# A two-layer graph network: attention formed inside the second edge pass, and gathered rows as three bf16 parts

## The chip, the cores and the metric

One core of a Trainium2 chip runs the kernel. The metric is device microseconds of one execution; the times of a kernel are given as the median of several runs. A profiled execution has a time of its own and a span, which is the time from its first to its last recorded instruction.

## The reference: what is computed

The graph has N = 12500 nodes with 256 features and E = 200000 edges (`src`, `dst`), sorted by `dst`. Two blocks follow each other, each with a residual:

```
h = relu(layernorm(x))
# block 1: two graph convolutions, self loops included
h = h @ W_pre + b_pre
h = relu(conv(h, W1, b1)); h = relu(conv(h, W2, b2))
x = x + h @ W_post + b_post          # conv: out[d] = sum over edges (s, d) of norm * (h @ W)[s]
# block 2: attention, 4 heads of 64
h = relu(layernorm(x)); xt = (h @ weight).reshape(N, 4, 64)
alpha = softmax over heads(leaky_relu(xt[src] . attn_l + xt[dst] . attn_r))
tmp[n] = sum over heads of alpha[n] * xt[dst[n]]      # alpha and dst of edge n, for n < N
x = x + tmp, repeated for each of the 4 heads
```

In block 2 only the first N edges count: node n takes the scores of edge n. As `dst` is sorted, the destinations of these 12500 edges are among the first nodes (under 1152), while their sources are spread over all nodes. So the term with `attn_l`, the left score, of an edge may belong to any node, also to one that is finished last.

## The kernel before: how the work is laid out

**Passes.** After a preparation (loads, degree counts, layer norms, a table of rows in DRAM, `table1`) come two edge passes, both made by `convolve` (L1153). Edges are cut into 112 chunks (`NCH`) of 14 tiles (`J`) of 128 edges, 1563 tiles in all. The loop at L1365 goes over tiles. For each tile GpSimd's queue (Pool) gathers 128 rows of the table by the edges' sources with one indirect DMA (L1374), and TensorE multiplies a one-hot matrix (`fhot`, made for a whole chunk by `one_hots`, L1239) by these rows and adds the product to `acc` in PSUM (L1382), f32 by f32. A row has 260 f32 (1040 bytes) in pass 1 and 256 (1024 bytes) in pass 2. Rows land in a ring of chunk buffers named `fgot`: five in pass 1 (`new_got`, L533), four in pass 2 (`new_rows_of`, L1251, with `ahead` 4). In pass 1 the first four chunks come from `x` itself, gathered in the preparation (L668).

**Windows.** A chunk's sums are turned and added (`close`, `turn`, `add`, from L1273) into a moving buffer over the sorted destinations. When a window of 128 nodes is complete, `shift` takes the steps that `finish` returned. There are 98 windows (`NT`). The steps of pass 1 are `finish1` (L1410): the weights, relu, and a row block stored to `table2` by ScalarE's queue (L1423). Those of pass 2 are `finish2` (L1464): the weights of the second convolution (L1472), W_post (L1488), the residual stored to `kept_x` (L1495), layer norm, a transpose (L1514), and the attention's products (L1527), from which the left scores go to DRAM tables `table_l` and `table_e` (L1536, L1538), and for the first nine windows (`XW`) the rows and right scores to `table_r`.

**Order.** The kernel is written with an order made by hand: every engine runs its instructions in the order of the program. A step is entered by `at` (L1167) with the tile count at which it is due, and `run(t)` (L1183) emits what is due behind each tile's matmul. So the work of windows is strewn between tiles. In the last chunks (`near`, L1278) the distances shrink to one tile a step. Waits follow from the tiles and tables that instructions read and write; the first chunk of pass 2 gathers only from `table[:(NT - TW) * P]`, the rows but for the last two windows, and edges with sources in these two are added by `late_sums` (L1256), which takes one chunk buffer of the ring.

**Attention.** Two groups' end rows are formed in the pass (`ends`, `copied`, L1551 and L1556). The rest comes behind the last window, in the block from L1605: for 15 groups of up to 7 node tiles, `ends_of` (L1638) forms the rows of destinations by products with one-hots `hot_t` (made by `turn_hots`, L1570, from destinations loaded to all partitions); `mix` (L1656) gathers the left scores with one indirect DMA a node tile (L1662, 98 in all), then softmax over heads, the weighted sum over heads on DVE (L1685 to L1692), the residual (L1694), and the store to `out` (L1700). For the first chunk of edges the sources in the last three windows are added by products (`missing`, L1627, with `hot_l`).

**Fallback.** Counts are checked on the chip; if one fails, `tile_preln_gcn_gat_kernel` (L1714) runs `general_path` behind the fast path.

Of the kernel before, what the change touches and what calls it, by code (L numbers as in the profile page):

```python
# [10 lines left out]
I32 = mybir.dt.int32  # L11
# [402 lines left out]
def fast_path(  # L414
# [57 lines left out]
    table2 = dram.tile([NT * P, D], F32, name="ftable2")  # L472
    kept_x = dram.tile([NT * P, D], F32, name="kept_x")
# [3 lines left out]
    assert AC * J == NT and AC * CE <= E and XW < NT  # L477
    table_r = dram.tile([XW * P, DR], F32, name="table_r")
    table_l = dram.tile([NT * P, H], F32, name="table_l")

    LW = 3
    table_e = dram.tile([NT * P, H], F32, name="table_e")
# [18 lines left out]
    base_b = const.tile([P, NCH], F32, name="base_b")  # L501
    row_i = const.tile([P, AC], I32, name="row_i")
# [88 lines left out]
    with tc.tile_pool(name="fprep", bufs=1) as prep:  # L591
# [233 lines left out]
        with tc.tile_pool(name="fpsum", bufs=2, space=PSUM) as psum, \  # L825
# [227 lines left out]
            wide = prep.tile([NCH, P], F32, name="wide")  # L1053
            nc.vector.tensor_copy(wide, base.to_broadcast([NCH, P]))
# [7 lines left out]
            nc.tensor.matmul(fk[:, 2, :NCH], wide, ident[:NCH, :NCH], start=True, stop=True)  # L1062
# [7 lines left out]
            for f in after:  # L1070
                f()
            after = [raw_block(ends, m, psum.tile([P, 4 * P], F32, name="ft"), j0)
                     for j0 in (8, 12)]
            nc.vector.tensor_copy(base_b, fk[:, 2, :NCH])
            nc.vector.tensor_scalar(row_i, base_b[:, :AC], lane, float(XW * P - 1), op0=ALU.add,
                                    op1=ALU.min)
# [16 lines left out]
    def check_chunks(work, psum):  # L1093
# [20 lines left out]
        kept = work.tile([1, 1], F32, name="n_kept", bufs=1)  # L1114
        nc.vector.tensor_reduce(kept, pt[:1, 2, :NCH], AX.X, ALU.add)
        nc.vector.tensor_add(kept, kept, counted)
        nc.vector.tensor_scalar(bad_row, kept, -1.0, float(NCH + 1), op0=ALU.mult, op1=ALU.add)
# [12 lines left out]
    def load_late(pool):  # L1130

        nc.scalar.dma_start(roots, root_t)
        for t, w in ((wb, w2), (wo, w_post), (wg[:, :, :D], w_gat)):
            nc.scalar.dma_start(t, w.rearrange("(k p) n -> p k n", p=P))
        nc.scalar.dma_start(b2c, b2.rearrange("(k p) -> p k", p=P))
# [8 lines left out]
    def late_weights(pool, attn):  # L1144

        for i, ar in enumerate(attn):
            for k in range(KC):
                prod = pool.tile([P, H, C], F32, name="fprod", bufs=1)
                nc.vector.tensor_mul(prod.rearrange("p h c -> p (h c)"), wg[:, k, :D], ar)
                nc.vector.tensor_reduce(wg[:, k, D + i * H:D + (i + 1) * H], prod, AX.X,  # L1150
                                        ALU.add)

    def convolve(ep, table, stride, width, ahead, with_sum, psum, prepare, finish, lacking=False,  # L1153
                 raw=(), rows_p=None):
# [28 lines left out]
        def run(now=None):  # L1183

            while due:
# [3 lines left out]
                do(d)  # L1189

# [41 lines left out]
        const_p = psum.tile([P, P if with_sum else P + D], F32, name="iota_p", bufs=1)  # L1232
        iota_p = const_p[:, :P]
        nc.vector.tensor_copy(iota_p, iota_w)
        if not with_sum:
            state["bias"] = const_p[:, P:]
            nc.vector.tensor_copy(state["bias"], bob)

# [4 lines left out]

        def hot_of(c):

            n = nj[c]
            h = ep.tile([P, J, P], F32, name="fhot", bufs=3)
# [3 lines left out]
        def new_rows_of():  # L1251
            if with_sum:
                return new_got()
            return rows_p.tile([P, J, stride], F32, name="fgot", bufs=ahead)

        def late_sums():  # L1256

            h = ep.tile([P, J, P], F32, name="fhot", bufs=3)
# [5 lines left out]
            px = psum.tile([P, KC, P], F32, name="fpt", bufs=1)  # L1264
# [8 lines left out]
        def close(c, acc, t):  # L1273
# [4 lines left out]
            near = c + 3 >= NCH  # L1278
# [20 lines left out]
            def shift(now):  # L1299
# [31 lines left out]
                for i, (o, step, fills) in reversed(list(enumerate(steps))):  # L1331
                    then = at(now + (i + 1 if near else o), lambda _, step=step: step(), fills, then)
# [32 lines left out]
        for t, (c, j) in enumerate(tiles):  # L1365
# [3 lines left out]
            if j == 0:  # L1369
                gots = (raw + [spare])[c] if raw and c <= len(raw) else new_rows_of()  # L1370
            got = gots[:, j, :]
            some = lacking and c == 0
            if c >= len(raw):
                nc.gpsimd.indirect_dma_start(  # L1374
                    out=got, out_offset=None, in_=table[:(NT - TW) * P, :] if some else table[:],
# [377 lines left out]
```

## Time and profile before

| | |
|---|---|
| median of 4 runs | 4150.29 us (4150.09 to 4151.45) |
| the profiled execution | 4146.63 us, its span 4144.8 us |
| Pool | 3103.8 us busy (75%), 3299 instructions |
| TensorE | 3096.9 us busy (75%), mean granted clock 0.799 |
| VectorE (DVE) | 1139.8 us busy (28%) |
| ScalarE (ACT) | 491.8 us busy (12%) |
| DMA | 554.57 MB, mean 134 GB/s |
| first tile gather (L1374) | 131.7 us |
| last tile gather ends | 3983.6 us |
| first and last score gather (L1662) | 4002.1 and 4125.4 us |

How to read it: a group's line names the source line, engine, operation, the tile written and those read, shapes and count; behind the bar stand the busy time, the mean duration in ns, and the idle time just before these instructions with what ended most of it ("issue": nothing that the profile shows). A timeline's line has start, duration, engine, line and operation, and in brackets the idle time before it and its releaser. PEld is the load of weights into TensorE; a name with q (SPq, ACTq, DVEq) is the engine's queue. Pool's indirect DMA is counted while descriptors are made; the transfer itself comes behind it.

### The profile page before, as it was taken

How to read it: one execution, taken by the hardware profiler on the slowest of the kernel's cores; microseconds unless marked ns; L12 is line 12 of the kernel's file. 1: busy time of each engine (PE TensorE's matmuls, PEld its weight loads, DVE VectorE, ACT ScalarE, POOL GpSimd, SP SyncE). 2: the span in 40 equal slices, each digit the busy share in tenths (PEclk: the TensorE clock that was granted, in tenths of full speed). 3: DMA queues.
4: the chain of work that ended last, by engine and by line, in shares of the span. 5: the costliest groups of instructions: out<-in, count | busy, mean ns of one | idle time of the engine just before them, and what ended most of it. 6: DMA issues, size and time to landing. Idle time of an engine off the chain costs nothing. (4 is left out here: it accounts for less than half of the span.)

```text
span 4144.8 us, 32267 instructions
## 1 busy us (share of the span) xinstructions
PE 3096.9 (75%) x10600; PEld 1970.8 (48%) x10600; DVE 1139.8 (28%) x2421; ACT 491.8 (12%) x1233; POOL 3103.8 (75%) x3299
## 2 busy tenths in 40 slices
PE   6688787877778888777587777777777777777774
PEld 5464443444444444444365555554555545555552
DVE  8632111111111111111232222222222222222238
ACT  5400000000000000000011111111111111111122
POOL 7677777777777777777777777777777777777766
PEclk7697878777887777778688888788888888888876
DMA  8644444444444444444545544555555445444556
GB/s 271 197 127 122 118 119 120 122 120 120 120 123 120 120 120 122 118 119 120 151 125 134 129 128 127 128 132 128 128 128 132 128 127 128 129 125 128 132 165 203
DMA packets 327419, 554.57 MB, mean 134 GB/s; under 512 B 96301, under 2 KB 224836, under 8 KB 327244
## 3 DMA queue, kind: packets, MB, share of 16 engines
q0 software_dynamic: 153520, 414.16, 37.7%
q1 hardware_dynamic: 127878, 121.99, 9.8%
q10 hardware_dynamic: 45846, 16.27, 1.6%
q8 instruction: 87, 1.43, 0.1%
q14 instruction: 88, 0.72, 0.1%
HBM read 498.89 MB, written 53.21 MB: 133 GB/s over the span
## 5 line engine op out<-in xcount | busy, mean ns | idle before, releaser
L1374 POOL DMA_INDIRECT fgot<-ftable,fsrc_t x3056 | 2892.4, 946 | 945.5 <-issue 885.5
L1382 PE MATMUL facc<-fgot,fhot 128*128 128x257 f32 (+1 forms) x6252 | 2344.0, 495 | 885.4 <-DMA fgot<-ftable,fsrc_t 839.6
L1382 PEld LDWEIGHTS facc<-fgot,fhot 128*128 128x128 f32 x6252 | 1261.5, 232 | 1806.9 <-DMA fgot<-ftable,fsrc_t 1366.3
L1293 DVE TENSOR_TENSOR buf<-buf,fturn 128x256 f32 x224 | 94.4, 422 | 1632.9 <-PE fturn L1206 1295.5
L1241 DVE TENSOR_TENSOR fhot<-iota_p,to_t 128x1792 f32<-128x1792 f32 x224 | 448.9, 2004 | 4.4 <-PE fpt L1267 4.4
L1479 DVE SCALAR_TENSOR_TENSOR fy<-rb,fb2c,fpz 128x128 f32<-128x128 f32 x194 | 58.7, 344 | 733.8 <-PE fpz L1472 732.9
L1276 ACT ACTIVATE fsums<-facc 128x257 f32<-128x257 f32 (+1 forms) x224 | 86.0, 384 | 1154.5 <-PE facc L1382 1145.0
L1493 DVE SCALAR_TENSOR_TENSOR fx<-fpo,fdinv,fxb 128x256 f32<-128x256 f32 x97 | 46.9, 483 | 484.9 <-PE fpo L1488 484.9
L1417 PE MATMUL fpo<-wf,buf 128*128 128x256 f32 x388 | 153.8, 539 | 0.3 <-DVE buf L1293 0.3
L1422 ACT ACTIVATE fo<-fpo,fdinv 128x256 f32<-128x256 f32 x97 | 45.9, 473 | 747.6 <-PE fpo L1418 745.8
L1417 PEld LDWEIGHTS fpo<-wf,buf 128*128 128x128 f32 x388 | 112.3, 290 | 28.7 <-DVE buf L1293 0.8
L1472 PE MATMUL fpz<-buf,fwb 128*128 128x128 f32 x776 | 122.9, 310 | 0.0
L1472 PEld LDWEIGHTS fpz<-buf,fwb 128*128 128x128 f32 x776 | 120.4, 233 | 2.2 <-DVE fy L1479 0.3
L1488 PE MATMUL fpo<-fwo,fz 128*128 128x256 f32 x388 | 111.5, 412 | 0.1
L1206 PE MATMUL fturn<-fident,self 128*128 128x128 f32 x396 | 83.8, 297 | 36.6 <-DMA to_all<-in_src_dram 24.1
L1662 POOL DMA_INDIRECT fal<-table_l,fsrc_t x84 | 81.1, 966 | 25.6 <-issue 22.6
L1206 PE MATMUL fturn<-fident,fsums 128*128 128x128 f32 x448 | 95.2, 298 | 0.5 <-ACT fsums L1276 0.5
L1652 PE MATMUL fends<-rows,hot_t 128*128 128x260 f32 x168 | 67.1, 565 | 35.3 <-ACT fxg L1654 34.9
L1518 ACT ACTIVATE ht<-fpt 128x256 f32<-128x256 f32 x97 | 37.1, 383 | 464.2 <-PE fpt L1514 464.2
L668 POOL DMA_INDIRECT fgot<-in_x_dram,raw_i x56 | 73.2, 1307 | 15.4 <-issue 15.3
L1206 PEld LDWEIGHTS fturn<-fident,fsums 128*128 128x128 f32 x448 | 69.6, 156 | 30.7 <-issue 7.4
L1418 PE MATMUL fpo<-bb,fins 2*128 2x256 f32 x194 | 82.5, 510 | 0.0
(267 smaller groups left out, 1716.8 us busy)
## 6 DMA issues: line engine op xcount, KB each, us to landing
fgot<-ftable,fsrc_t POOLq DMA_INDIRECT x3056
self<-ftable SPq DMA_DIRECT2D x99, 128.0 KB
self<-ftable SPq DMA_DIRECT2D x97, 130.0 KB
ftable<-fo ACTq DMA_DIRECT2D x98, 128.0 KB
kept_x<-fx SPq DMA_DIRECT2D x98, 128.0 KB
fxb<-in_x_dram SPq DMA_DIRECT2D x97, 128.0 KB
fxr<-kept_x SPq DMA_DIRECT2D x13, 896.0 KB
out_dram<-fres SPq DMA_DIRECT2D x13, 896.0 KB
```

Of the source, the lines that this page charges most:

```text
L668: nc.gpsimd.indirect_dma_start(out=raw[c][:, j, :D], out_offset=None, in_=x[:], in_offset=bass.IndirectOffsetOnAxis(ap=raw_i[:, k:k + 1], ...
L1206: nc.tensor.transpose(v["pt"][:, i * KC + k, :], rows[:, k * P:(k + 1) * P], ident)
L1241: nc.vector.tensor_tensor(h, iota_p[:, None, :].to_broadcast([P, n, P]), to[:, :, None].to_broadcast([P, n, P]), ALU.is_equal)
L1276: nc.scalar.activation(sb, acc, AF.Copy)
L1293: nc.vector.tensor_add(b, b, v["pt"][:, :KC, :])
L1374: nc.gpsimd.indirect_dma_start(out=got, out_offset=None, in_=table[:(NT - TW) * P, :] if some else table[:], in_offset=bass.IndirectOffset ...
L1382: nc.tensor.matmul(acc, hots[c][:, j, :], got[:, :width], start=(j == 0), stop=(j == nj[c] - 1 and not some))
L1417: nc.tensor.matmul(po, buf[:, k, :P], wf[:, k, :], start=(k == 0), stop=False)
L1418: nc.tensor.matmul(po, fs, bb, start=False, stop=True)
L1472: nc.tensor.matmul(pz[:, m, :], wb[:, k, m * P:(m + 1) * P], buf[:, k, :P], start=(k == 0), stop=(k == KC - 1))
L1488: nc.tensor.matmul(po, v["z"][:, m, :], wo[:, m, :], start=(m == 0), stop=(m == KC - 1))
L1662: nc.gpsimd.indirect_dma_start(out=al[:, i, :], out_offset=None, in_=(table_l if c else table_e)[:], in_offset=bass.IndirectOffsetOnAxis(a ...
```

## The change

1. **Rows in parts.** `finish1` now leaves each row of `table2` also as three bf16 parts (value, rest, rest of the rest) in `parts2`; pass 2 gathers from there (1536 bytes a row) and multiplies each tile's one-hots, now bf16, by the three parts. In pass 1 `split_rows` does the same for `table1`, one window in three tiles from tile 70 on, into `parts1` (1560 bytes a row); chunks from the 29th on (`SINCE` = 28) use it. The ring of pass 2 has three chunk buffers in place of four.
2. **Attention by products.** Left scores stay on the chip (`l_all`); `table_l` and `table_e` are gone. `start_of` is a load of a register on SyncE's queue. An edge's left score is taken in five stages of windows (`STAGES`), when they are complete, by a product of a one-hot of the source's place with the scores of a stage's windows, masked by the window's number (`alpha_l`); right scores by a product with end rows loaded from `table_r` (`ends_of_tile`, `alpha_r`). The softmax follows, and the weighted sum over heads is one product a node tile with weights spread by `pick` (`group`). The items stand in a list (`attend`) and are fed behind tiles by `feed`, each with a condition on the finished windows.
3. **Late edges at the end.** Of the first 12500 edges those with a source in the last 14 windows (from `LATE` = 84 on) are listed in pass 1 (`list_late`) on 16 lists of 128. Their end rows and one-hots are formed in pass 2 and kept in DRAM (`late_ends`, `late_hots`). Behind pass 2 their scores are completed, and their result rows, gathered from `kept_x`, replace rows of `out` by 16 scatters.
4. **Later transposes in pass 2.** The steps of `finish2` from the transpose on come 6 tiles later, and the four PSUM buffers of its steps become two (`fX`, `fY`). The shrunk distances of steps begin one chunk earlier (`soon`).

The core of the diff:

```diff
@@ convolve @@
-            return rows_p.tile([P, J, stride], F32, name="fgot", bufs=ahead)
+            return rows_p.tile([P, J, 3 * stride], BF16, name="fgot", bufs=ahead)
...
+        def feed(t):
+            if behind and t >= free_at[0] and behind[0][0]():
+                _, space, parts = behind.pop(0)
+                for i, part in enumerate(parts):
+                    if part:
+                        at(t + i, lambda _, part=part: part())
+                free_at[0] = t + space
...
-            nc.tensor.matmul(acc, hots[c][:, j, :], got[:, :width], start=(j == 0),
-                             stop=(j == nj[c] - 1 and not some))
+            for i in range(many):
+                nc.tensor.matmul(acc, hots[c][:, j, :], got[:, i * stride:i * stride + width],
+                                 start=(j == 0 and i == 0),
+                                 stop=(j == nj[c] - 1 and i == many - 1 and not some))
@@ finish1 @@
-            o = work.tile([P, D], F32, name="fo", bufs=3)
-            nc.scalar.activation(o, v["po"], AF.Relu, scale=dinv2[:, w:w + 1])
+            nc.scalar.activation(po, po, AF.Relu, scale=dinv2[:, w:w + 1])
+            v["parts"] = work.tile([P, 3, D], BF16, name="fparts", bufs=2)
+            nc.scalar.activation(v["parts"][:, 0, :], po, AF.Copy)
+            o = work.tile([P, D], F32, name="fo", bufs=2)
+            nc.scalar.activation(o, po, AF.Copy)
             nc.scalar.dma_start(table2[w * P:(w + 1) * P, :], o)
+    def to_parts(p, b, table, w):
+        nc.vector.tensor_tensor(p, p, b[:, 0, :], ALU.subtract)
+        nc.vector.tensor_copy(b[:, 1, :], p)
+        nc.vector.tensor_tensor(b[:, 2, :], p, b[:, 1, :], ALU.subtract)
+        nc.sync.dma_start(table[w * P:(w + 1) * P, :], b.rearrange("p i d -> p (i d)"))
@@ attend @@
+        def ends_of_tile(t):
+            at = start_of(t, (XW * P - NB) * H)
+            nc.sync.dma_start(ends[:, t, :], by_head[bass.ds(at, P), :])
@@ attend, alpha_l @@
+                for j in range(G):
+                    nc.tensor.matmul(v["p"][:, j, :, :], v["h"][:, j * P:(j + 1) * P],
+                                     l_all[:, w0:w1, :], start=True, stop=True)
@@ attend, group @@
+            return [load, None, equal, product, taken, lambda: v["soft"][0](),
+                    lambda: v["soft"][1](), turn, turned, over(0, 4), weigh(0, 4), over(4, G),
+                    weigh(4, G), mix, end]
...
+        for s in range(len(STAGES) - 1):
+            for b in range(NG):
+                items.append((when("w", STAGES[s][1]), 4, alpha_l(s, b)))
+        for b in range(NG):
+            items.append((when("w", LATE), 8, group(b)))
+        for t0, n in ((LATE, G), (LATE + G, 4), (LATE + G + 4, 3)):
+            items.append((when("x", t0 + n), 1, rest(t0, n)))
@@ behind pass 2 @@
+    def late_loads():
+            nc.sync.dma_start(sets["hot"], late_hot)
+            nc.sync.dma_start(sets["end"], late_end[:].rearrange("(k p) d -> p k d", p=P))
+    def fetch_x(most):
+            nc.gpsimd.indirect_dma_start(
+                out=sets["x"][:, k, :], out_offset=None, in_=kept_x[:min(LIMITS[k] * P, N), :],
+                in_offset=bass.IndirectOffsetOnAxis(ap=late_i[:, 1, k:k + 1], axis=0))
...
+        for k in range(KL):
+            nc.tensor.matmul(z[k // 8][:, k % 8, :, :], sets["hot"][:, k * P:(k + 1) * P],
+                             l_all[:, LATE:, :], start=True, stop=True)
...
+        for n in [2, 2] + [4] * ((KL - 4) // 4):
+            nc.vector.tensor_mul(near, heads[:, k, :, :C],
+                                 share[:, k, :, None].to_broadcast([P, n, H, C]))
+            nc.vector.tensor_reduce(mix, near.rearrange("p k h c -> p k c h"), AX.X, ALU.add)
+            nc.vector.tensor_tensor(res, res, mix[:, :, None, :].to_broadcast([P, n, H, C]),
+                                    ALU.add)
+            for i in range(k0, k0 + n):
+                nc.gpsimd.indirect_dma_start(
+                    out=out[:], out_offset=bass.IndirectOffsetOnAxis(ap=late_i[:, 0, i:i + 1],
+                                                                     axis=0),
+                    in_=sets["x"][:, i, :], in_offset=None)
```

## The prediction

> **What bounds the kernel now.** I read the costliest groups first, then Pool's timeline, then the busy time by stage, then the last 160 us.
>
> ```profile
> L1374 POOL DMA_INDIRECT fgot<-ftable,fsrc_t x3056 | 2892.4, 946 | 945.5 <-issue 885.5
> L1382 PE MATMUL facc<-fgot,fhot 128*128 128x257 f32 (+1 forms) x6252 | 2344.0, 495 | 885.4 <-DMA fgot<-ftable,fsrc_t 839.6
> ```
>
> Pool spends 946 ns on each gather and about 0.30 us before the next, waiting for nothing that shows. TensorE idles 885 us, 840 of it until a gathered row has landed. Pool is the metronome, TensorE follows. The seam of the passes on Pool:
>
> ```profile
> 2019.65 0.94 POOL L1374 DMA_INDIRECT fgot<-ftable,fsrc_t  x1 [0.30 <-issue]
> 2020.89 0.95 POOL L1374 DMA_INDIRECT fgot<-ftable,fsrc_t  x1 [0.30 <-issue]
> 2023.99 0.94 POOL L1374 DMA_INDIRECT fgot<-ftable,src  x1 [2.15 <-DMA ftable<-fo]
> 2025.24 0.95 POOL L1374 DMA_INDIRECT fgot<-ftable,src  x1 [0.30 <-issue]
> ```
>
> The period is 1.25 us. 1507 gathers of pass 1 and 1563 of pass 2 at 1.2508 us are 3840 of the 4144.8 us. Between the two middle lines Pool waits for a stored row of the table.
>
> ```profile
> 2500.00:3000.00 500.00, 359.93 (x1341) 251.08 (x1342) 132.22 (x280) 59.91 (x161) 378.17 (x401) 0.82 0.51 129
> 4000.00:4145.00 145.00, 78.70 (x262) 51.18 (x261) 108.16 (x202) 35.62 (x104) 94.61 (x98) 0.68 0.67 211
> ```
>
> (Stretch, length, busy PE, PEld, DVE, ACT, Pool; clock, DMA share, GB/s.) In pass 2 only Pool has a full beat: 401 instructions in 500 us. The last stretch is attention alone:
>
> ```profile
> 3982.68 0.95 POOL L1374 DMA_INDIRECT fgot<-ftable,fsrc_t  x1 [0.31 <-issue]
> ...
> 4002.11 0.94 POOL L1662 DMA_INDIRECT fal<-table_e,fsrc_t  x1 [10.98 <-ACT fxl L1535]
> ...
> 4125.35 0.94 POOL L1662 DMA_INDIRECT fal<-table_l,fsrc_t  x1 [0.30 <-issue]
> ...
> 4138.34 0.66 SPq L1703 DMA_DIRECT2D out_dram<-fres  x1
> ```
>
> Call the end of the last tile gather L (3983.63). The tail is 161.2 us: 18.5 until the last window's left scores exist, 124 for 98 gathers of scores, the rest for the last group and its store.
>
> **Rows in three bf16 parts.** A tile's matmul becomes three bf16 ones. In the same warm stretch of the trace:
>
> ```profile
> 151.75 1.03 PE L1382 MATMUL facc<-fgot,fhot 128*128 128x257 f32 x4
> 152.75 0.49 PE L567 MATMUL fpt<-lohi_t,parts_d 128*98 128x256 bf16 x3
> ```
>
> Four f32 instructions (two tiles) take 1.0 us, three bf16 ones 0.33 until the next begins: a tile falls from 0.50 to 0.33 us. That is 0.17 x 2734 tiles = 465 us of TensorE, worth nothing in time, since TensorE was waiting; it makes room. Pool's side: as many gathers, of 1536 or 1560 bytes a row. The trace has 966 ns for rows of 16 bytes and 946 for 1024 and 1040; I take no change (bounds: below nothing is excluded, as the instruction is the same; above, in proportion to bytes, 473 ns). The DMA share, 0.51 at 129 GB/s, goes with 1.5 times the gathered bytes and the new loads to some 200 GB/s, or 0.79 by proportion: room left. Making the parts (98 steps, one in three tiles: two ACT of 0.39, three DVE of 0.42, a load and a store) uses 1.3 of 3.75 us of a DVE that is 18% busy there: hidden. The first parts gather is 25 tiles (31 us) behind the last step, and TensorE runs 3 us behind Pool: no wait.
>
> **The seam.** The rows of pass 2 now pass two more ACT copies and three DVE instructions before they are stored: 2.0 us more, and the first gather waits for just that. Gone are five hot_t and hot_l instructions with both sides in SBUF, four of which stretched a gather (periods of 1.72, 1.73, 1.92 and 2.12 us, 2.5 too much), and one ring wait of 2.2. The ring has three chunks, one lent to late_sums, so the 29th gather waits for chunk 0. TensorE begins pass 2 at 2068.9 now, behind loads that the change drops; I put it at 2048 and the end of chunk 0 at 2062, the gather being due at 2061: 2 us (0 to 20). Sum: 2.0 + 2.0 - 2.5 - 2.2 = -0.7.
>
> **Attention behind pass 2.** Each of 14 alpha_r, 56 alpha_l and 14 group items issues 7 to 21 small products. L1633 gives 0.146 us an instruction (42 in 6.12), two to a product. The tight stage is the groups, 8 tiles or 10.0 us each. TensorE: 0.33 + 0.24 (windows and turns) a tile is 4.6; 43 instructions are 6.3; together 10.9. DVE: base 0.33 a tile, 2.6; equal over 896 elements 1.2 (1.09 ns an element by L1685); the alpha product's mask and sum 1.45; softmax 1.2; weighing 1.4; adding to the kept rows 2.0 by L1694; together 9.9. So both run at or just over the beat for 112 tiles and TensorE falls 13 us or more behind; the ring hides 28 tiles (35 us), and 40 tiles follow to catch up in. I take 3 us (0 to 60).
>
> Sync gets one register load and one transfer a tile for 98 tiles:
>
> ```profile
> L1288 DVEq TENSOR_LOAD <-offs x224: 298/303/556, 175.6 to 3988.6; - x112
> ```
>
> With 0.1 for address arithmetic and 0.5 for the issue that is 0.9 of 1.25 us: hidden. The Trainium skill ("DMA: Bandwidth & Descriptors", "Latency and other measured facts") gives a register load a floor of about 600 ns; with it Sync would be at 1.2 of 1.25, and the loads of the windows would come late by a few us, within the ring.
>
> **The tail, from L.** Gone: the 98 gathers of scores. The last l_all is at L+18.0 as now. 32 instructions of products at 0.146: L+22.7. The second bank's mask and sum 1.3, softmax with eight steps of 0.22: L+25.8. The first pair's three DVE steps of 0.69: L+27.9. Beside it 3.1 MB of late lists load on Sync's queue from L+8; at the 271 GB/s of the page's first slice they take 11.6 us, ahead of the last kept_x stores, then the last three rows load (3), add (0.95) and store (3.1): L+28.5. Eleven of the 16 row gathers run by L+18, five from L+21 to L+27. So the first scatter goes at L+28.5.
>
> Sixteen scatters follow. Each is declared on the whole output, and the trace shows how accesses to one DRAM table are ordered: by declared rows, with Pool held until the store has landed. So I take each scatter to wait for the landing of the one before. No scatter is in the trace; bounds for one: 2.85 us, as a gather from its start (2018.40) to its matmul (2021.25); 4.1, 0.95 of issue and the 3.14 from the end of ACT's store issue (2020.85) to the gather it held. I take 3.4, nearer the gather, which has its queue. 15 x 3.4 + 0.95 = 52: L+80.5. From the end of the last store's issue to the span's end is 5.8 now: L+86.3. The tail loses 161.2 - 86.3 = 74.9 us.
>
> The skill's same page ("Two DMAs through the same engine are not ordered") speaks against a scatter at the end: one queue orders nothing, only the completion semaphore does. Its fit for Pool's transfers (2.0 us plus bytes at 436 GB/s) would make a scatter an estimated 0.95 + 2.3 = 3.25 us, and the sum 2 us less.
>
> **Sum.** -74.9 - 0.7 + 3 = -72.6 us on the profiled execution's 4146.63 (span 4144.8): 4074.0. The median of the runs shown, 4150.29, is 3.7 above it: **4078**.
>
> **Rivals.** (a) The forecast, 4078: chance 0.48. (b) Scatters not chained: 16 x 1.25 = 20 in place of 52, so 32 less: **4046**. For it: Pool's gathers never wait for one another; against: the held gather above. Chance 0.23. (c) The groups fall further behind, 13 us each: 42 us of lag, 7 past the ring and some 15 left at L: **4100**; at 16 us 4135. For it: 10.9 and 9.9 of 10.0 above, with both engines in order; against: the slack before and after. Chance 0.15. (d) **Slower**: a gather of 1536 bytes holds Pool longer, in its issue or because transfers back up. It decides from 72.6 / 2734 = 27 ns a gather; a tenth of 946 would be 259 us: **4337**. Against it: the equal times for 16 and 1040 bytes; for it: nothing in the trace is longer than 1040. Chance 0.12. (e) The change doesn't run: a count fails and the general path follows, far over twice the time. Its limits (a list of at most 2048 late edges, 1707 in these inputs, 128 rows a list) hold. Chance 0.02.
>
> **Numbers.** (a) to (c) reach from about 4036 to 4125 when (c) is cut at its middle; outside lie (d), (e) and part of (c), under 2 in 10. About 0.2% (8 us) is what a measurement here tells from no change: faster 0.85, same 0.02 (the far end of (c)), slower 0.13.
>
> **What would show it.** Pool's period stays 1.25 us in both passes, with no stretch of waits near the groups; the L1374 count stays 3056; tile matmuls three to a tile and shorter; the gather that opens pass 2 about 2026; L between 3980 and 3995; sixteen scatters 3 to 4 us apart with the DMA as releaser in (a), 1.25 apart in (b). A period over 1.27 us makes (d); Pool waiting on TensorE in the last 150 tiles makes (c).

## The result, and the profile after

The kernel after the change takes 4156.98 us (median of 32 runs), the kernel before 4150.36 (52 runs): a ratio of 1.0013, with a 95% interval of 1.0008 to 1.0018. The forecast was 4078; the change gains nothing. Nine of the eighteen experiment runs below fell on two chips (0 and 2 in the record, "the slow chips" from here on) on which the kernel before takes 4.93 ms instead of 4.15; their times are set only beside the kernel before on the same chip.

The profiled execution has a span of 4151.2 us (4144.8 before). First the two costliest groups of the page of the kernel after:

```profile
L1414 POOL DMA_INDIRECT fgot<-parts,fsrc_t x2720 | 2574.7, 947 | 892.8 <-issue 800.2
L1424 PE MATMUL facc<-fgot,fhot 128*128 128x256 bf16 (+2 forms) x8986 | 1853.0, 349 | 884.5 <-DMA fgot<-parts,fsrc_t 858.7
```

A gather of 1536 or 1560 bytes a row holds Pool for 947 ns, as one of 1024 did (946), and the median distance of two gathers is still 1.251 us. TensorE still waits 859 us for rows (840 before). So far the picture of before. The seam of the passes, in Pool's timeline of the kernel after:

```profile
2023.55 0.95 POOL L1414 DMA_INDIRECT fgot<-parts,fsrc_t  x1 [0.30 <-issue]
2028.74 0.94 POOL L1414 DMA_INDIRECT fgot<-parts,src  x1 [4.25 <-PE facc L1424]
```

Pass 1 ends 2.7 us later than before; the step to pass 2 is 5.19 us instead of 3.10. The profile also names another releaser: before it was the landing of the table's last rows (`DMA ftable<-fo`), now it is TensorE's last product of pass 1. From there Pool keeps its beat for 106 chunks. Then come the groups of attention, and with them six waits at the starts of chunks. From the waits of the kernel after between 3850 and 4050 us (what waited, for whom: us in all, times, the longest):

```profile
POOL fgot L1414 <- PE facc L1424: 65.7, 6, 18.6
...
ACT turned_a L2083 <- PE behind L2078: 31.4, 8, 5.4
...
DVE weights L2096 <- PE behind L2089: 23.3, 9, 4.0
DVE hot_s L1931 <- DMA lo_all<-lo_rows: 21.4, 9, 5.9
```

Pool waits for TensorE to free a chunk buffer: 63.8 us more than the beat in six gaps. At the last tile gather (its end, called L in the prediction, is at 4047.8 instead of 3983.6) TensorE is another 19.7 us behind. And TensorE, VectorE and ScalarE wait for each other. One group in TensorE's timeline, from one `mix` (line 2104) to the next:

```profile
3898.40 3.23 PE L2104 MATMUL behind<-ends_all,weights 128*128 128x64 f32 x14
...
3904.39 0.37 PE L2078 MATMUL behind<-fident,al_all 128*28 128x128 f32 x1 [1.47 <-DVE al_all L1896]
...
3907.68 2.07 PE L2089 MATMUL behind<-turned_a,pick 28*128 28x128 f32 x8
...
3911.92 1.64 PE L2089 MATMUL behind<-turned_a,pick 28*128 28x128 f32 x6
3913.50 3.22 PE L2032 MATMUL behind<-l_all,hot_s 128*128 128x48 f32 x14
...
3918.22 3.09 PE L2104 MATMUL behind<-ends_all,weights 128*128 128x64 f32 x14
```

19.8 us for a group that is fed every 8 tiles, that is every 10.0 us of Pool's beat; the mean of the 13 distances is 17.2. The rows left out are tiles' matmuls and windows. In these rows 14 instructions of lines 2032 and 2104 take 3.1 to 3.2 us, 0.22 to 0.23 each; the granted clock is 0.50 from the first row to the last.

The tail, in Pool's timeline:

```profile
4060.61 0.94 POOL L2205 DMA_INDIRECT fgot<-kept_x,late_i  x1 [0.30 <-issue]
4083.68 0.94 POOL L2205 DMA_INDIRECT fgot<-kept_x,late_i  x1 [22.13 <-DMA kept_x<-fx]
...
4094.36 1.01 POOL L2249 DMA_INDIRECT out_dram<-fgot,late_i  x1 [4.73 <-DVE fgot L2246]
4097.09 0.97 POOL L2249 DMA_INDIRECT out_dram<-fgot,late_i  x1 [1.72 <-DMA out_dram<-fgot,late_i]
```

The first scatter starts at L + 46.6, the sixteen are 2.91 us apart in the mean. Thirteen of the fifteen that follow are held by the landing of the one before; for two the profile names a result of VectorE as the last wait. The execution ends 13.3 us after the last has started. What stands there is the closing of Pool's queue. First the kernel before, then the kernel after (shortest, median and longest in ns, first and last start):

```profile
L1749 POOLq DRAIN  x3: 40/107/4242, 4129.4 to 4144.5; - x3
```

```profile
L2291 POOLq DRAIN  x3: 40/107/6937, 4143.4 to 4150.9; - x3
```

Before, the long DRAIN (4.24 us from 4129.4) ran while the other engines were at the last group. After, it takes 6.94 us and begins 5.5 us after the last scatter, when the other engines have nothing left to do. Why it is longer is open.

The tail is 103.4 us, where it was 161.2. So the tail gives 57.8 us, the groups take 63.8, and 0.3 is left for all else: the span grows by 6.4.

### The profile page after: what moved, and what is told of

It is laid out like the page before. It is cut to its first block, busy times and chain, and to the rows that moved or that the text cites. A ratio compares the mean times of both kernels' runs of the same rounds, so it can differ in the third digit from the quotient of the medians.

```text
span 4151.2 us, 42986 instructions
## 1 busy us (share of the span) xinstructions
PE 2881.1 (69%) x14818; PEld 2084.8 (50%) x14818; DVE 1608.1 (39%) x3483; ACT 624.0 (15%) x1627; POOL 3032.8 (73%) x3226
## 5 line engine op out<-in xcount | busy, mean ns | idle before, releaser
L1414 POOL DMA_INDIRECT fgot<-parts,fsrc_t x2720 | 2574.7, 947 | 892.8 <-issue 800.2
L1424 PE MATMUL facc<-fgot,fhot 128*128 128x256 bf16 (+2 forms) x8986 | 1853.0, 349 | 884.5 <-DMA fgot<-parts,fsrc_t 858.7
L1424 PEld LDWEIGHTS <-fhot 128*128 128x128 bf16 x8202 | 971.0, 120 | 1436.1 <-issue 1184.7
L1265 DVE TENSOR_TENSOR fhot<-iota_p,to_t 128x1792 bf16<-128x1792 f32 (+1 forms) x224 | 449.2, 2006 | 0.0
L1414 POOL DMA_INDIRECT fgot<-ftable,fsrc_t x336 | 318.1, 947 | 117.7 <-issue 104.8
L2032 PE MATMUL behind<-l_all,hot_s 128*128 128x72 f32 (+1 forms) x980 | 158.2, 327 | 92.1 <-DVE hot_s L1931 56.5
L2032 PEld LDWEIGHTS behind<-l_all,hot_s 128*128 128x128 f32 x980 | 150.2, 241 | 104.7 <-issue 76.8
L1424 PEld LDWEIGHTS facc<-fgot,fhot 128*128 128x128 f32 x784 | 169.9, 225 | 55.6 <-issue 12.5
L1813 PE MATMUL fX<-buf,fwb 128*128 128x128 f32 x776 | 158.2, 372 | 1.6 <-DVE buf L1327 1.5
L1813 PEld LDWEIGHTS fX<-buf,fwb 128*128 128x128 f32 x776 | 151.0, 288 | 8.0 <-DVE buf L1327 2.4
```

Of the source, the lines that this page charges most:

```text
L1265: nc.vector.tensor_tensor(h, iota_p[:, None, :].to_broadcast([P, n, P]), to[:, :, None].to_broadcast([P, n, P]), ALU.is_equal)
L1414: nc.gpsimd.indirect_dma_start(out=got, out_offset=None, in_=rows_of[:(NT - TW) * P, :] if some else rows_of[:], in_offset=bass.IndirectOf ...
L1424: nc.tensor.matmul(acc, hots[c][:, j, :], got[:, i * stride:i * stride + width], start=(j == 0 and i == 0), stop=(j == nj[c] - 1 and i == ...
L1813: nc.tensor.matmul(pz[:, m, :], wb[:, k, m * P:(m + 1) * P], buf[:, k, :P], start=(k == 0), stop=(k == KC - 1))
L2032: nc.tensor.matmul(v["p"][:, j, :, :], v["h"][:, j * P:(j + 1) * P], l_all[:, w0:w1, :], start=True, stop=True)
```

## The experiments

The theories. T1: TensorE's own work is too much for the beat at the clock that it is granted. T2: the groups are a chain of dependent steps and its length is the price, however busy the engines are. T3: the clock follows the load, so that less work is paid back by a lower clock. T4: the DMA engines; either their bandwidth (T4a) or the order in Sync's queue (T4b). All kernels start from the kernel after. "Waits" are Pool's in the gaps of the last chunks, beyond the beat; "group" is the mean distance of two mixes; "clock" is the mean granted clock from about the first group to TensorE's last tile; "lag" is the time from the start of the last gather to the start of TensorE's last product on gathered rows. All in us, from the profiled executions; ratios are to the kernel before, with 95% intervals.

| kernel | median | ratio | waits | group | clock | lag |
|---|---|---|---|---|---|---|
| after | 4157.0 | 1.0013 (1.0008 to 1.0018) | 63.8 | 17.2 | 0.71 | 19.7 |
| one_part_again | 4152.7 | 1.0009 (0.9999 to 1.0018) | 62.4 | 16.8 | 0.56 | 21.0 |
| thin_rows | 4146.9 | 0.9995 (0.9985 to 1.0004) | 55.3 | 16.2 | 0.57 | 22.3 |
| f32_late | 4156.2 | 1.0017 (1.0006 to 1.0029) | 64.3 | 17.0 | 0.72 | 21.5 |
| queue_only_again | 4170.8 | 1.0050 (1.0033 to 1.0067) | 76.7 | 17.8 | 0.65 | 19.5 |
| deep | 4158.9 | 1.0020 (1.0011 to 1.0030) | 65.0 | 17.2 | 0.73 | 23.5 |
| deep_over | 4140.9 | 0.9982 (0.9972 to 0.9991) | 45.5 | 15.6 | 0.76 | 23.1 |
| deep_over_early | 4128.8 | 0.9947 (0.9930 to 0.9963) | 48.5 | 16.1 | 0.75 | 9.4 |
| act_queue | 4100.2 | 0.9889 (0.9871 to 0.9907) | 16.5 | 13.6 | 0.80 | 5.9 |
| act_space10 | 4091.6 | 0.9864 (0.9846 to 0.9882) | 1.1 | 14.3 | 0.81 | 19.4 |

**Less work for TensorE.**

```diff
-            for i in range(many):
+            used = 1 if not with_sum and c >= 92 else many
+            for i in range(used):
```

> From pass 2's chunk 92 on only the first of the three bf16 parts is multiplied (the two others are gathered and left out of the sum, so the rows there have bf16 precision). Theory T1: the groups hold Pool because TensorE's own instructions, at the granted clock of 0.5 to 0.7, make 16.3 us of 8 tiles and a group where the gathers make 10.0. A tile costs 0.75 us there, so 8 tiles lose 4.0 us: 12.3 us a group, 14 x 2.3 = 32 us of lag, inside the ring's 42 tiles (52 us). The 64 us of Pool's waits go, TensorE is not 19.5 us behind at the last gather but some 3: 64 + 16 less, about 4077 us. T2: the groups are a chain of 15 steps over TensorE, VectorE and ScalarE, each waiting for the one before, in two banks; the length of the chain is the price and TensorE's share of work does not matter: 4150 to 4160 us, waits of Pool still near 64 us.

> The same kernel as one_part, because the chip of the first four runs made 4928 us of the kernel before and TensorE there often took 0.70 us from one instruction to the next. The theories and their numbers stay: T1 (TensorE's own work at the granted clock) about 4077 us; T2 (the chain of waits) 4150 to 4160 us, on a chip where the kernel before takes 4150 us.

The first run fell on a slow chip: 1.0367 (1.0338 to 1.0395) of the kernel before there. The second gave 4152.7 us, waits 62.4. TensorE had two of a tile's three instructions less over 20 chunks, and the groups are as slow as before. Two stretches of 10 us of the kernel after, then the same of one_part_again (busy PE, PEld, DVE, ACT, Pool; clock, DMA share, GB/s):

```profile
3810.00:3820.00 10.00, 8.61 (x69) 7.18 (x67) 6.51 (x17) 0.80 (x3) 7.56 (x9) 1.00 0.72 217
3870.00:3880.00 10.00, 10.00 (x45) 8.71 (x45) 3.97 (x8) 0.42 (x1) 7.56 (x9) 0.50 0.98 313
```

```profile
3810.00:3820.00 10.00, 9.49 (x43) 8.21 (x42) 5.40 (x14) 0.80 (x3) 7.56 (x9) 0.50 0.78 228
3870.00:3880.00 10.00, 9.31 (x42) 8.28 (x42) 4.94 (x12) 0.42 (x1) 7.56 (x9) 0.50 1.01 329
```

And the whole stretch of the groups, again after and then one_part_again:

```profile
3803.00:4066.00 263.00, 222.97 (x1273) 189.79 (x1271) 140.89 (x307) 50.06 (x111) 147.48 (x156) 0.71 0.77 240
```

```profile
3803.00:4062.00 259.00, 215.34 (x963) 182.76 (x963) 139.59 (x301) 48.96 (x107) 146.28 (x154) 0.56 0.78 242
```

The clock is full or half, and with less work it is half nearly throughout (0.56 against 0.71 in the mean). So the number of TensorE's instructions is not the price: 310 fewer, and T1's 4077 us did not come. But T1 is not refuted by this run. TensorE is recorded busy for 215.3 us instead of 223.0: most of what was saved went into the lower clock (T3), so its time hardly fell. What speaks against T1 comes below.

**Fewer bytes.**

```diff
+            nc.scalar.dma_start(first2[w * P:(w + 1) * P, :], v["parts"][:, 0, :])
...
-                    out=got, out_offset=None,
+                    out=got[:, :stride] if thin else got, out_offset=None,
+                    in_=first2[:] if thin else
```

> As one_part (from pass 2's chunk 92 on only the first bf16 part is multiplied, the others left out of the sum), and there the gathers also fetch only that part: 512 bytes a row from a table of its own instead of 1536. TensorE's, VectorE's and ScalarE's work is that of one_part, which changed nothing; only the bytes differ. T4 (the DMA engines are what the groups run into: 1.57 MB of gathered parts, 0.92 loaded of kept rows, 0.92 stored, 0.45 of lists and 0.2 of the windows make 4.1 MB in 8 tiles, 410 GB/s on the beat, where no 10 us of the trace has more than 360; the loads of lo_all come late behind them): 3.0 MB a group, 12 us or less, Pool's waits 0 to 15 instead of 64, less lag at the end: 4075 to 4100 us. T2 or T1 (chain, TensorE): 4150 to 4157 us.

Measured 4146.9 us, waits 55.3: 5.8 us below one_part_again (the intervals of the two ratios just overlap), with a DMA share of 0.57 in the stretch instead of 0.78. The bytes may cost something, but T4a, which asked for 4075 to 4100, is not the answer. The other way to fewer bytes:

```diff
+            if since == 0 and many == 1:
+                got = gots.rearrange("p j d -> p (j d)").bitcast(F32)
+                got = got[:, j * stride:(j + 1) * stride]
...
-            many = 1 if c < since else 3
+            many = 1 if c < since or (since == 0 and c >= 92) else 3
```

> Computes the same. From pass 2's chunk 92 on the gathers fetch f32 rows of 1024 bytes from table2, as before the change, with f32 one-hots, two f32 passes a tile instead of three bf16 ones. T4: 3.6 MB a group instead of 4.1, some 14 us: Pool's waits fall from 64 to 25 to 45 us, 4115 to 4140 us. T1: TensorE has 0.25 us a tile more to do, 2 us a group: 4175 to 4190 us. T2: no change, 4150 to 4160.

Measured 4156.2, waits 64.3, as after. The edit does two things that pull opposite ways, more work for TensorE and a third fewer bytes, and it leaves the one-hots of pass 2 two buffers instead of three. Together they come to nothing: TensorE is recorded busy for 235.2 us of the stretch instead of 223.0, and the groups are no slower (17.0). So in the groups' stretch the bf16 parts are worth nothing in time, as forecast.

**The order of the steps.** The steps of a group, in tiles from its start:

```diff
-            return [load, None, equal, product, taken, lambda: v["soft"][0](),
-                    lambda: v["soft"][1](), turn, turned, over(0, 4), weigh(0, 4), over(4, G),
-                    weigh(4, G), mix, end]
+            steps = {0: load_lo, 5: equal, 7: product, 8: load, 9: scores, 11: lambda: v["soft"][1](),
+                     13: turn, 14: turned, 16: over(0, 4), 17: weigh(0, 4), 18: over(4, G),
+                     19: weigh(4, G), 21: mix, 22: end}
+            return [steps.get(i) for i in range(23)]
```

> Computes the same with the same instructions; only the order of a group's 15 steps is stretched from 15 to 23 tiles (loads of lo_all 5 tiles ahead, two tiles or one between a product and its reader), so that nearly three groups are in flight and a step rarely waits for the one issued just before it. T2 (the chain of dependent steps is the price, one_part_again spoke for it): 16.3 us a group falls to what TensorE's own work needs, 12 to 14 us; lag of 28 to 56 us, Pool's waits from 64 to 0 to 20, less lag at the end: 4085 to 4125 us. T1 (TensorE's own work at the granted clock): no change, 4150 to 4160 us. T3 (the clock answers to the load, so that less or smoother work is paid back by a lower clock): waits go but the clock falls, 4140 to 4157 us.

Measured 4158.9 us: no gain, which is T1's number and not T2's. Its trace shows another reason. Sync's queue, then VectorE's row that waits for it:

```profile
3915.83 0.57 SPq L2057 DMA_DIRECT2D fxr<-kept_x  x1
3916.45 0.56 SPq L1925 DMA_DIRECT2D lo_all<-lo_rows  x1
```

```profile
3929.15 1.09 DVE L1931 SCALAR_TENSOR_TENSOR hot_s<-lo_all,iota_p 128x896 f32<-128x896 bf16 x1 [9.17 <-DMA lo_all<-lo_rows]
```

The load of `lo_all` (0.22 MB) is issued behind the load of a group's kept rows (0.92 MB) on the same queue, and VectorE can use it only 12.7 us later. In this kernel VectorE waited 40.4 us for it between 3850 and 4050, instead of 21.4: the time that the wider order took away from one wait went to the next.

> Computes the same. deep, with line 2089's products as 7 bf16 instructions on three stacked parts instead of 14 f32 ones (as in over_bf16). T2: once the chain is off the path TensorE's work counts, 3.1 us a group less at half clock: 10 to 12 us a group, no or few waits of Pool, lag at the last gather under 10 us: 4070 to 4090 us. T1: 4090 to 4110. T3: as deep, 4140 to 4157.

```diff
-    pick = ap.tile([G * H, G, P], F32, name="pick")
+    pick = ap.tile([96, G, P], BF16, name="pick")
...
-                nc.tensor.transpose(v["p"][:G * H, :P], al[:, t, :].rearrange("p t h -> p (t h)"),
-                                    ident)
+                nc.tensor.matmul(v["p"][:96, :P], al_3.rearrange("p i k -> p (i k)"), ident_b,
+                                 start=True, stop=True)
```

Measured 4140.9: 18 us less than deep, where 70 to 90 were expected. So fewer products in the group do help, where fewer tile matmuls in one_part did not; that this is because the products stand in the chain was not tested. The number lies in T3's range (4140 to 4157), but the clock did not fall (0.76 against deep's 0.73). The early start comes next:

```diff
+            quick = not with_sum and 93 <= c <= 96
...
-            at(t + (2 if c + 1 == NCH else 3 if near else 13), add)
+            at(t + (2 if c + 1 == NCH else 3 if near or quick else 13), add)
```

> Computes the same. deep_over, and the windows that complete in chunks 93 to 96 go through their steps in 18 tiles instead of 34 and are added 3 tiles after their chunk instead of 13, so that the scores of window 83 exist and the groups begin 26 tiles (32 us) sooner, in a stretch where TensorE is 3 us behind Pool. Under all theories TensorE then has 60 instead of 34 tiles after the groups to catch up: lag at the last gather about 3 us, the first scatter near L + 28.5: 0 to 16 us less than deep_over, 4065 to 4085 us.

Measured 4128.8, 12 us less; the lag falls from 23.1 to 9.4, the waits stay (48.5). The expected 0 to 16 us less came; the expected 4065 to 4085 rested on deep_over's forecast.

**Sync's queue.**

```diff
-                v["row"] = row_of(lo_rows, b, "lo_all", 1)
+                v["row"] = row_of(lo_rows, b, "lo_all", 2, nc.scalar)
```

> Computes the same. deep_over_early (4129 us), with the loads of lo_all on ScalarE's DMA queue and with two buffers. In deep_over_early its packets stood behind a load of 0.92 MB on Sync's queue and took 12.5 us from the first to the last. T4b (the order in Sync's queue is the price): lo_all lands in 3 to 5 us, Pool's waits fall from 48 to 10 to 25: 4095 to 4115 us. T4a (the engines as such are full): the bytes are the same, 4122 to 4132 us.

Measured 4100.2 us, 28.5 less than deep_over_early, with the same instructions and the same bytes. The edit changes two things, the queue and the number of buffers of `lo_all` (two instead of one). The waits of deep_over_early from 3770 to 4030, then those of act_queue from 3770 to 4000:

```profile
POOL fgot L1415 <- PE facc L1425: 48.9, 5, 12.0
...
DVE hot_s L1935 <- DMA lo_all<-lo_rows: 46.9, 11, 10.4
```

```profile
POOL fgot L1415 <- PE behind L2105: 8.4, 1, 8.4
POOL fgot L1415 <- PE facc L1425: 8.1, 2, 4.8
...
DVE hot_s L1935 <- DMA lo_all<-lo_rows: 0.2, 1, 0.2
```

VectorE's wait for `lo_all` goes from 46.9 us to 0.2 and Pool's from 48.5 beyond the beat to 16.5; a group takes 13.6 us instead of 16.1. That speaks against T1 and for T4b. No run has the second buffer alone in this order, but the trace of deep_over_early tells the two apart: in its last eleven groups, the ones that waited, the load of `lo_all` is issued 6.0 to 8.5 us after VectorE has read the buffer for the group before, so it was not the buffer that held it; in ten of them it follows the load of the kept rows on Sync's queue by 0.4 to 1.1 us. The Trainium skill ("DMA: Bandwidth & Descriptors", "Queues, rings and completion order") says that each DMA engine takes turns between the queues that have work, and that Sync and ScalarE have a queue each; the fall from 46.9 to 0.2 us agrees with it, though it does not show the turns themselves. Is the queue then the cause by itself? The same edit on the kernel after:

> Computes the same. The kernel after with one edit: the loads of lo_all go on ScalarE's DMA queue, with two buffers. If Sync's queue is the cause by itself (T4b alone), VectorE's 21 us of waits for lo_all go and with them most of Pool's: 4095 to 4125 us. If the short chain of dependent steps holds the groups as well (T2 with T4b), only some of it goes: 4135 to 4152 us.

> The same kernel as queue_only: the kernel after, with the loads of lo_all on ScalarE's DMA queue and two buffers. The queue by itself (T4b alone): 4095 to 4125 us. Short chain of dependent steps as well (T2 with T4b): 4135 to 4152 us, with Pool's waits still 35 us or more.

The first run fell on a slow chip: 1.0477 (1.0445 to 1.0509) of the kernel before there. The second gave 4170.8 us, 14 more than after and above both forecast ranges. Its waits between 3850 and 4050:

```profile
POOL fgot L1414 <- PE facc L1424: 73.9, 6, 19.3
...
DVE hot_s L1931 <- DMA lo_all<-lo_rows: 29.6, 11, 3.8
```

In the short order the load is due only two tiles ahead of its reader, and now ScalarE issues it, behind the step `turned` that itself waits for TensorE. The longest wait for `lo_all` falls from 5.9 to 3.8 us, but there are eleven of them. So neither the order nor the queue gains alone; in act_queue, which has both, and the bf16 products and the early start, the queue is worth 28.5. Order and queue without the other two:

> Computes the same. deep with the loads of lo_all on ScalarE's DMA queue and two buffers; line 2089 stays in f32 and the groups start where they did. T2 with T4b: both waits go, 12 to 14 us a group, Pool's waits 10 to 35 us: 4105 to 4135 us, clearly below both deep (4159) and queue_only. T4b alone: as queue_only. T1 (TensorE's own work is the next limit): 13 us or more a group, upper end.

> The same kernel as deep_queue: the stretched order of the steps and the loads of lo_all on ScalarE's queue with two buffers, f32 products, groups starting where they did in the kernel after. If the two waits hide each other (each step waits for the longer of the step before and lo_all), both together give what neither gave: act_queue's 29 us below deep_over_early, so about 4130 us, Pool's waits near 35 us; 4110 to 4140. If the gain of act_queue hangs on the bf16 products or the early start, 4145 to 4170.

Both fell on slow chips: ratios of 1.0445 (1.0414 to 1.0475) and 1.0318 (1.0237 to 1.0399) to the kernel before there. Pool waits there at over 100 of the 111 starts of chunks within pass 2, so they tell nothing of the groups. Whether the queue's gain needs the bf16 products or the early start stays open.

**The version that the results point to.** One number: a group every 10 tiles.

> Computes the same. act_queue with a group every 10 tiles instead of every 8, which the 26 tiles gained by the early start pay for: 14 groups end at tile 1542 of 1563. By T4a a group's 2.5 MB then share 12.5 us with 10 tiles' 1.96 MB: 357 GB/s instead of 410; lag grows slower, about 14 x 1 to 2.5 us = 14 to 35 us, within the ring: Pool's waits 0 to 15 and 10 to 30 us less than act_queue, 4080 to 4105 us. By T1 and T2 as well the groups get 2.5 us more each; this run is for the best version, not to tell the theories apart.

Measured 4091.6 us, 0.9864 (0.9846 to 0.9882) of the kernel before and the fastest here. Pool's waits in the groups are gone (1.1) and L is 3988.1, inside the forecast's 3980 to 3995; the lag of 19.4 us is back, since the groups now end at the last tiles. The wait on the last kept rows shows it:

```profile
POOL fgot L2227 <- DMA kept_x<-fx: 24.7, 1, 24.7
```

> Computes the same. act_space10 (4092 us) with a group every 9 tiles and the steps of windows 80 to 83 one tile apart, so that the groups begin 9 tiles sooner and end 23 sooner. In act_space10 Pool waited 1 us, but TensorE was 19 us behind at the last gather and the first scatter came at L + 50. With 44 tiles left after the groups the lag falls to 3 to 8 us; Pool's waits rise to 0 to 8: 4075 to 4090 us.

It fell on a slow chip: 1.0427 (1.0391 to 1.0464) of the kernel before there; no verdict.

**The scatters.**

```diff
-                    out=out[:], out_offset=bass.IndirectOffsetOnAxis(ap=late_i[:, 0, i:i + 1],
+                    out=apart[i][:], out_offset=bass.IndirectOffsetOnAxis(ap=late_i[:, 0, i:i + 1],
```

> The 16 scatters of the tail go each into a DRAM table of its own instead of the output, so that none is declared on the same memory as another; the late rows are thus left out of the output. If the waits between them are the declared order on one table, they come 1.25 us apart, as gathers do, instead of 2.87: 15 x 1.6 = 24 us less, 4133 us. If the queue or the store itself spaces them, or VectorE's steps feed them, the time stays at 4157 us or falls by under 8.

> The same kernel as apart: the 16 scatters go each into a DRAM table of its own, so the late rows are left out of the output. Chained by the declared order on one table: they come 1.25 us apart instead of 2.9, 24 us less than the kernel after, 4133 us. Spaced by the queue or the store itself, or fed slower by VectorE (a four-list step of 3.6 us there feeds four scatters, so it would bind only below 0.9 us each): 4150 to 4157 us.

These kernels leave the late rows out of the output. Both runs fell on slow chips (1.0346, 1.0316 to 1.0376, and 1.0424, 1.0394 to 1.0455, of the kernel before there), so the whole time says nothing; but the distances of the scatters can be read. Pool's timeline of apart_again:

```profile
5100.15 0.98 POOL L2250 DMA_INDIRECT apart<-fgot,late_i  x1 [0.31 <-issue]
5101.43 0.97 POOL L2250 DMA_INDIRECT apart<-fgot,late_i  x1 [0.30 <-issue]
5102.71 0.97 POOL L2250 DMA_INDIRECT apart<-fgot,late_i  x1 [0.30 <-issue]
```

The sixteen are 1.32 us apart in the mean; in the other kernels on the same chip (queue_only, deep_queue, act_space9) 2.91. So it is the declared order on one table that spaces them, 15 x 1.59 = 24 us of the tail.

**Two more runs**, on a slow chip as well, without a verdict: the earlier load of `lo_all` on Sync's queue (1.0413, 1.0384 to 1.0441) and the bf16 products in the short order (1.0340, 1.0309 to 1.0371).

```diff
-            return [load, None, equal, product, taken, lambda: v["soft"][0](),
+            return [load_lo, None, None, None, None, None, load, None, equal, product, taken,
+                    lambda: v["soft"][0](),
```

> In the groups the load of lo_all gets two buffers and is issued five tiles earlier, ahead of the rest of the group's loads. Computes the same. T2 (chain of waits): VectorE waited 21 us for lo_all between 3850 and 4050, TensorE behind it; 20 to 27 us of Pool's waits go, 4130 to 4137 us. T1 (TensorE's own work): TensorE only moves its idle time elsewhere, 0 to 8 us less, 4149 to 4157 us.

> The spreading of the weights over nodes and heads (line 2089) is done with the weights as three bf16 parts stacked on 96 partitions: 7 bf16 instructions for 14 f32 ones, and one bf16 product for the transpose, against 4 small VectorE steps more (0.8 us) in every group. Computes the same. T1: TensorE loses 3.7 + 0.4 - 1.0 = some 3.1 us a group at half clock: 13.2 us a group, 45 us of lag, at the ring's edge; Pool's waits fall from 64 to 0 to 15 us and the lag at the end by 10 or more: 4085 to 4105 us. T2: the chain is 0.8 us longer in VectorE and 2 shorter in TensorE: 4140 to 4160 us.

## Why the prediction was wrong, step by step

- **Pool as the metronome: right.** The beat is 1.251 us in both passes, the gathers take 947 ns. Rival (d), the longer gather, did not come.
- **Parts worth nothing in time: right.** TensorE waits no less for rows than before (859 us against 840), and f32_late shows no gain from them in the tight stretch.
- **The seam: near, by luck in part.** The step between the passes is 2.1 us longer, 2.0 was forecast, but the profile names TensorE's last product as the releaser and not the stored rows. Pass 1 ends 2.7 us later, which was not forecast, and the 2 us at the 29th gather did not come. L without the groups' waits would be 3984.0, so all of this comes to +0.3 us against -0.7.
- **Sync: right for the loads of end rows.** The 98 register loads and transfers of end rows ran in 116 us, 1.19 each, under the beat, with register loads of 0.27 us and no wait of Pool. The prediction did not follow what Sync does in the groups.
- **"Groups in pass 2: I take 3 us": the step that failed.** It cost 63.8 us of waits and 14.6 of further lag at L (19.7, where the kernel before has 5.1 by the same measure): 78.4 us in place of 3, and the median missed by 79. The step summed each engine's busy time by itself, 10.9 for TensorE and 9.9 for VectorE per 10.0 us, and let the ring hide the rest. A group took 17.2 us. In the row of the whole stretch above TensorE is busy for 223.0 of 263 us and VectorE for 140.9, which makes 14.6 and 9.2 us a group: VectorE's term was near, TensorE's was 3.7 short, and for another 2.6 us a group TensorE was not busy at all. Two things are behind this. The products were priced at 0.146 us, a row at a mean clock of 0.75; at half clock 14 of them took 3.1 to 3.2 us (0.22 each), at full clock 1.7. And the steps depend on each other, within a group and through Sync's queue, where `lo_all` stands behind the kept rows: with TensorE's instructions unchanged a group fell from 16.1 to 13.6 us when that load moved to another queue. How the 7.2 us beyond the beat divide between clock, chain and queue in the kernel after stays open. Rival (c) had the mechanism and its sign in the profile ("Pool waiting on TensorE in the last 150 tiles"); it was mis-sized, at 13 to 16 us a group. With 17.2 its arithmetic holds: 14 groups fall 101 us behind, 35 of them in the ring, and the 66 left are close to the 63.8 that Pool waited.
- **The tail: half right.** First scatter at L + 46.6 instead of L + 28.5; 14.6 of the 18.1 us are the lag. Sixteen scatters chained, as in the forecast; (b) is rejected by the releasers, and apart_again shows what it would have given. They cost 2.91 us instead of 3.4 (7.4 less). The end behind the last one took 6.5 more than was carried over from the last store, since Pool's DRAIN of 6.94 us now comes last (in apart_again it is as long, so it is not the chain). That these two nearly cancel is luck.
- **The register loads.** The Trainium skill ("DMA: Bandwidth & Descriptors", "Latency and other measured facts") gives a floor of about 600 ns; the trace has 0.27 us (median of 114), so the prediction's own sum of 0.9 us was the better one.

What act_space10 makes of it: with the groups off Pool's path the gain of the tail comes through, 59.5 us of the forecast 72.6.

## What to carry to other kernels

For work that is threaded between the steps of a full engine, don't only add up busy time per engine: write down the chain of one item across engines and queues, with the clock that the stretch will have, and compare it with how many items are in flight. A small load that starts such a chain belongs on a queue where nothing large stands ahead of it, and early enough; here neither the order nor the queue gained alone. When removing one wait changes nothing, look which wait has grown in its place before giving up the theory. When removing work changes nothing, look whether the clock has fallen before calling the work free. And what closes a program's last queue may have been hidden behind other engines: moving that queue's work to the end uncovers it.

## What the runs showed of the hardware

- TensorE's clock stands at half in a stretch in which it is recorded as busy all the time (3870 to 3880: 45 instructions, 10.00 us, 0.50), and at full in one where 69 instructions fill 8.61 us. The Trainium skill ("TensorE: Matmul & The Clock Gate", Part 1) has the clock rise after about 3.4 us of sustained work; the row of 10 us speaks against it, though a busy time is modelled.
- A scatter followed the one before on the same table after 2.66 to 3.38 us (2.91 in the mean), on a table of its own after 1.27 to 1.32 where VectorE did not hold it.
- Pool's DRAIN at the end of the program took 6.94 us where scatters came last and 4.24 us in the kernel before.
- Exp and Sqrt in turn cost ScalarE a table load of 1.28 us each: 17 from 3791.7 on in the kernel after, where the kernel before has one (at 4007.5). None was in the forecast, and no run tells what they cost the groups.
- Chips differ: on the two that take 4.93 ms for the kernel before, TensorE often needs 0.70 us or twice that from one instruction to the next, with nothing in the trace that it waits for. In apart 399 of the distances between weight loads lie between 0.64 and 0.76 us (about 110 in the kernel after on another chip). From its timeline:

```profile
3035.64 0.27 PE L1425 MATMUL facc<-fgot,fhot 128*128 128x256 bf16 x1 [0.94 <-issue]
3036.37 0.38 PE L1425 MATMUL facc<-fgot,fhot 128*128 128x256 bf16 x1 [0.47 <-issue]
3037.08 0.37 PE L1425 MATMUL facc<-fgot,fhot 128*128 128x256 bf16 x1 [0.32 <-issue]
```

  The versions with the change's attention were 3.2 to 4.8% slower than the kernel before there. Why those chips do this is open.
